# Gated cross-attention with an expert layer on one NeuronCore: another beginning, unpadded queries, context as 128 and 64 rows

## The chip, the core and the metric

The kernel runs on one core of one Trainium2 chip. The time is the device time of one execution in microseconds; the kernel before takes 589.01 us (median of three runs, 587.1 to 589.69). The profile is one further execution, taken with the hardware profiler. TensorE multiplies matrices, VectorE (DVE) reduces and combines, ScalarE (ACT) applies functions and copies, GpSimd (POOL) does small work and indirect DMA, SyncE (SP) issues DMA.

## The reference

For 16 sequences of 112 tokens of 256 numbers, and for each a context of 375 rows of 192 numbers:

```python
x = x + tanh(g_xattn) * xattn(layernorm(x), ctx, mask, Wq, Wk, Wv, Wo)
x = x + tanh(g_ffn) * ffn(layernorm(x), router_w, gate_w, gate_b, up_w, up_b, down_w, down_b)

# xattn: 16 heads of 16 numbers
q, k, v = x @ Wq, ctx @ Wk, ctx @ Wv            # split into heads
attn = softmax(where(mask, q @ k.T * 16**-0.5, -max))
return (attn @ v) @ Wo

# ffn: 8 experts of 512, the best two for each token
probs = softmax(x @ router_w.T)                  # two largest kept, made to sum to 1
h = silu(x @ gate_w[e] + gate_b[e]) * (x @ up_w[e] + up_b[e])
return sum over the two of probs[e] * (h @ down_w[e] + down_b[e])
```

All is float32.

## The kernel before

**Batches.** The main loop takes step i = 0 to 15, one for each batch, as a pipeline: step i holds the keys of batch i + 1, the values and score maxima of batch i, the scores, exponentials and weighted sums of batch i - 1, and the projection, second norm and routing of batches i - 2 to i - 4. The list `order` (L670) writes the order of these pieces down, `first_order` (L711) that of step 0; before them stands a prologue (L681 to L710). All engines but POOL run in the written order (`manual_schedule`, L164), so a waiting instruction holds up everything behind it on its engine, DMA issues included.

**Heads in row groups.** A head has 16 numbers. In `k_sb` and in the query tile `q1` each head has 32 rows: 16 of data, row 16 for the row maximum, row 17 for the mask. Four heads lie above each other, in four groups (NG). A score product has 32 rows, and products on different 32-row groups of TensorE run at the same time.

**Keys** (L362) are `wk.T @ context`, with the 192 context rows as two pieces of 96 (CC): for each half of the heads two products. ScalarE copies the result to `kc`, and eight DMAs spread its heads to their 32-row places in `k_sb` (three buffers; their other rows are filled once, by `set_keys`, and the mask rows by `masks`). **Values** (L386) are three products of 125 context positions, also in two pieces of 96 rows. **Queries** (L330) use `wqp`, the query weights with each head padded to 32 columns, so that the product comes out in its 32-row places; VectorE adds `row_mask` as it evicts it.

**Maxima and scores.** `maxima` (L403) multiplies keys and queries, and VectorE reduces each pair of heads to row maxima in `mt`. `q_less_max` (L426) transposes `mt` on TensorE and subtracts it from the queries, so that the next product needs only an exponential. `scores` (L443) gives the transposed scores, and ScalarE their exponential. `both` (L466) merges a unit of scores of one batch with a unit of maxima of the next. Each unit takes one of two buffers (`ps_s`). So two such groups follow each other no sooner than the exponential and the reduction of the first are done; pieces between them are TensorE's cover. All other products share three PSUM buffers (`ps_m`), which go around.

**Memory queues.** `fetch(i)` (L652) puts the loads of a later context, mask rows and tokens on SP, and two expert weight loads of 512 KB on ScalarE's queue. `load_more` (L201) loads the gates, `wo`, router and biases and clears two buffers; the tanh of the gates (L851) is the first ScalarE instruction of step 1. Eight semaphores tell of landed DMAs of both queues; a DMA that is given one in use waits for the landing of the earlier DMA.

**Experts.** Tokens are sorted into blocks of 128 for one expert. Twelve blocks (NA) from the first 11 batches are planned inside the loop, the rest at the end of the attention by `plan_rest` (28 small VectorE steps, L950). The blocks' work is a list of pieces: for each block `begin` (gate product, turn of the next block), `up`, and `others` (lists, gathers, `down` of two blocks before, `turn_h` of one before). `blocks(n)` (L1163) runs the next n pieces; between them stands the rest of the attention, and at L1231 the plan, ten steps and then one piece. After it come the lists of blocks 12 to 15 and their gathers.

## Time and profile before

| what | value |
|---|---|
| median of three runs | 589.01 us (587.1 to 589.69) |
| profiled execution | 583.11 us, span 581.3 us |
| mean granted TensorE clock | 0.986 |
| TensorE busy | 541.6 us, 93% of the span |
| VectorE, ScalarE, POOL busy | 353.4, 215.5, 143.4 us |
| DMA | 64.49 MB, 111 GB/s |
| first reduction of score maxima | at 23.11 us |
| transposes of batch 0's maxima (step 1), of batch 6's and 7's | at 34.42, 184.00 and 205.61 us |

The span is the time from the first to the last instruction. A line of a timeline gives the start in the span, the time that the merged instructions cover, the engine (a q behind it: its sequencer, which issues DMAs), the line of the kernel, the operation, the tiles (result, then operands), the number of instructions, and in brackets how long the engine had been idle and what released it. A float32 product shows as two TensorE passes. A group's line gives busy time, the mean ns of one instruction, and the idle time before it.

### The profile page before, as it was taken

What the parts mean: (1) busy time and instruction counts of PE and PEld (TensorE: products, weight loads), DVE (VectorE), ACT (ScalarE), POOL (GpSimd) and SP (SyncE); (2) the same over time, 40 slices, a digit from 0 to 9 for tenths busy, and PEclk for the clock granted to TensorE, in tenths of its full rate; (3) what the DMA queues carried; (4) which work ended last, traced back from release to release, by engine and by line L of the source; (5) the groups of instructions that cost most, each with busy time, mean ns of one, the idle gap of its engine ahead of it and who ended that gap; (6) DMA issues with size and microseconds to landing.
All of it is one profiled execution on the core that took longest, in us unless ns stands there. A gap on an engine that the chain in (4) does not pass through costs nothing. (4 is left out here: it accounts for less than half of the span.)

```text
span 581.3 us, 13620 instructions
## 1 busy us (share of the span) xinstructions
PE 541.6 (93%) x5159; PEld 381.8 (66%) x5159; DVE 353.4 (61%) x883; ACT 215.5 (37%) x391; POOL 143.4 (25%) x187
## 2 busy tenths in 40 slices
PE   3999999999999999999999999999979999999990
PEld 2567777777777777777776676666546666666660
DVE  4464656676676677666666765566884646464640
ACT  2334443533533533443444344423223333333320
POOL 6000000210210210110110123254543354425432
PEclk9999999999999999999999999999979999999996
DMA  4355244244154154144211107555645566677421
GB/s 116 83 149 138 63 140 127 45 137 133 39 139 133 39 137 127 42 124 131 52 38 42 37 11 226 134 118 108 155 101 166 147 167 144 176 244 189 91 27 21
DMA packets 45810, 64.49 MB, mean 111 GB/s; under 512 B 12456, under 2 KB 36464, under 8 KB 45680
## 3 DMA queue, kind: packets, MB, share of 16 engines
q1 hardware_dynamic: 29152, 41.79, 25.1%
q0 software_dynamic: 7168, 8.42, 9.8%
q10 hardware_dynamic: 9424, 13.38, 7.5%
q8 instruction: 43, 0.70, 0.5%
q14 instruction: 23, 0.19, 0.1%
HBM read 48.87 MB, written 10.01 MB: 101 GB/s over the span
## 5 line engine op out<-in xcount | busy, mean ns | idle before, releaser
L420 DVE TENSOR_REDUCE mt<-s 112x2 f32<-112x750 f32 x128 | 118.5, 938 | 72.3 <-PE s L411 72.0
L462 ACT ACTIVATE pt<-st 125x896 f32<-125x896 f32 x96 | 88.0, 917 | 111.5 <-PE s L411 108.3
L411 PE MATMUL s<-k,q 32*112 32x375 f32 x512 | 125.2, 518 | 0.4 <-DVE mt L420 0.2
L452 PE MATMUL st<-q,k 32*125 32x112 f32 x1536 | 108.2, 279 | 9.0 <-DVE mt L420 5.5
L452 PEld LDWEIGHTS st<-q,k 32*125 32x125 f32 x1536 | 91.2, 183 | 28.3 <-DVE mt L420 15.9
L1042 DVE TENSOR_TENSOR gu<-gu,b 128x512 f32<-128x512 f32 x64 | 41.3, 686 | 70.3 <-PE gu L1026 70.3
L1081 PE MATMUL pd<-wd,hT 128*128 x256 | 62.7, 389 | 3.7 <-ACT hT L1073 3.7
L1081 PEld LDWEIGHTS pd<-wd,hT 128*128 128x128 f32 x256 | 49.4, 195 | 22.5 <-issue 11.9
L636 POOL DMA_INDIRECT routed<-ent,slot x32 | 31.1, 971 | 128.5 <-DVE slot L632 123.7
L1026 PE MATMUL gu<-wg,xT 128*128 x128 | 61.2, 601 | 0.2 <-issue 0.2
L411 PEld LDWEIGHTS s<-k,q 32*112 32x112 f32 x512 | 54.8, 170 | 9.5 <-DVE mt L420 7.5
L1026 PE MATMUL gu<-wu,xT 128*128 x128 | 60.6, 596 | 0.0
L297 POOL TENSOR_TENSOR rstd<-ve,mhalf 112x1 f32<-112x1 f32 x32 | 18.4, 574 | 160.7 <-DVE ve L295 160.7
L390 PE MATMUL vp<-wv_sb,c 96*125 96x256 f32 x192 | 52.6, 396 | 0.0
L368 PE MATMUL kp<-c,wk_sb 96*128 96x375 f32 x128 | 49.3, 512 | 0.0
L1051 ACT ACTIVATE sg<-gu 128x512 f32<-128x512 f32 x32 | 20.2, 631 | 74.8 <-DVE gu L1042 74.8
L482 PE MATMUL o<-pt,v 125*32 125x112 f32 x1536 | 46.8, 262 | 0.0
L482 PEld LDWEIGHTS o<-pt,v 125*32 125x32 f32 x1536 | 35.2, 110 | 13.9 <-issue 13.7
L838 POOL DMA_INDIRECT x<-normed,toks x32 | 32.6, 1017 | 34.0 <-issue 22.9
L390 PEld LDWEIGHTS vp<-wv_sb,c 96*125 96x125 f32 x192 | 33.2, 187 | 9.8 <-issue 6.1
L1026 PEld LDWEIGHTS gu<-wg,xT 128*128 128x128 f32 x128 | 22.5, 194 | 16.7 <-issue 16.6
L1026 PEld LDWEIGHTS gu<-wu,xT 128*128 128x128 f32 x128 | 21.9, 191 | 15.4 <-issue 15.4
(170 smaller groups left out, 654.9 us busy)
## 6 DMA issues: line engine op xcount, KB each, us to landing
b<-bias_d SPq DMA_DIRECT2D x32, 640.0 KB
k<-kc SPq DMA_DIRECT2D x124, 46.9 KB
c<-in_ctxT_dram SPq DMA_DIRECT2D x32, 140.6 KB
wg<-in_gate_w_dram ACTq DMA_DIRECT2D x8, 512.0 KB
wu<-in_up_w_dram ACTq DMA_DIRECT2D x8, 512.0 KB
wd<-in_down_w_dram ACTq DMA_DIRECT2D x8, 512.0 KB
xs<-in_x_dram SPq DMA_DIRECT2D x16, 112.0 KB
total<-xs SPq DMA_DIRECT2D x16, 112.0 KB
```

Source lines behind the costliest of these rows:

```text
L368: nc.tensor.matmul(ps[:, :M], lhsT=wk_sb[:, k, j * 128 : (j + 1) * 128], rhs=c[:, k, :], start=(k == 0), stop=(k == 1),)
L390: nc.tensor.matmul(ps[:KC, :D], lhsT=ct[:, k, c * KC : (c + 1) * KC], rhs=wv_sb[:, k, :], start=(k == 0), stop=(k == 1),)
L411: nc.tensor.matmul(ps[:N, j, :M], lhsT=q1[rows, g, (b % 2) * N : (b % 2 + 1) * N], rhs=kt[rows, g, :], start=True, stop=True,)
L420: nc.vector.reduce_max(mt[:, g, 2 * rp : 2 * rp + 2, R_MAX], ps[:N, :, :M], axis=AX.X)
L452: nc.tensor.matmul(ps[:KC, j, g * N : (g + 1) * N], lhsT=kt[rows, g, c * KC : (c + 1) * KC], rhs=q2[rows, g, :], start=True, stop=True,)
L462: nc.scalar.activation(pt, ps[:KC, :, : NG * N], AF.Exp)
L482: nc.tensor.matmul(o[32 * r : 32 * r + 32, g * N : (g + 1) * N], lhsT=vt[:, c, 2 * g + rp, j : j + 2, :].rearrange("p t d -> p (t d)"), rh ...
L636: ins = nc.gpsimd.indirect_dma_start(out=routed, out_offset=bass.IndirectOffsetOnAxis(slot[:, k : k + 1], 0), in_=s["ent"][:, k, :], in_of ...
L838: nc.gpsimd.indirect_dma_start(out=bs[j]["x"], out_offset=None, in_=normed[: FIRST * N] if j < NA else normed, in_offset=bass.IndirectOffs ...
L1026: nc.tensor.matmul(s["ps"][:, i, :F], lhsT=s["xT"][:, k, :], rhs=w[:, bass.ds(s["e"], 1), k, :].rearrange("p o f -> p (o f)"), start=(k == 0),
L1042: nc.vector.tensor_tensor(s["gu"][:, i], s["ps"][:, i, :F], s["b"][:, i * F : (i + 1) * F], ALU.add)
L1081: nc.tensor.matmul(pd[:, :D], lhsT=s["hT"][:, f, :], rhs=wd[:, bass.ds(s["e"], 1), f, :].rearrange("p o d -> p (o d)"), start=(f == 0), st ...
```

## The change

- Context, `wk` and `wv` are loaded as 128 rows and 64 rows, and the 64 rows stand twice, in rows 0 to 63 and 64 to 127 of the tile. The last steps of two products (two halves of the keys, two chunks of values) then lie on different halves of TensorE's rows. Values are made as chunks 0 and 1 together and chunk 2 alone.
- Queries of batches 2 on use the weights as they are; VectorE copies the product, and eight DMAs a batch spread its heads. Two query buffers are filled once with `row_mask`. Batches 0 and 1 keep the padded way, with the padded weights in buffers of the exponentials.
- The prologue loads and works off keys ahead of norms, POOL too runs in the written order there, eight products of the identity with itself stand first on TensorE, `set_keys` runs on VectorE and POOL instead of ScalarE, and `load_more` moves from the prologue's end to step 1, behind its `fetch`.
- The pieces of a step stand in another order, in step 0 too.
- `plan_lanes` moves to the beginning of the last part, and the plan goes in sevens instead of tens.

```diff
-CC = C // 2
+CW = C - 128
...
+    early = ExitStack()
+    early.enter_context(tc.manual_schedule(engines={POOL}))
...
+    def load_wide(tile, rows, part, q=nc.sync):
+        if part == 0:
+            q.dma_start(out=tile[:, 0, :], in_=rows[:128])
+        else:
+            for i in range(2):
+                q.dma_start(out=tile[i * CW : (i + 1) * CW, 1, :], in_=rows[128:])
+
     def load_ctx(b):
-        c = a2.tile([CC, 2, M], F32, name=f"c_{b}", tag="c", bufs=3)
...
+        ctx_tiles[b] = a2.tile([128, 2, M], F32, name=f"c_{b}", tag="c", bufs=3)
+        for part in range(2 if b else 0):
+            load_wide(ctx_tiles[b], ctxT[b], part)
...
     load_ctx(0)
-    stage_q = ac.tile([128, KD, D], F32, name="stage_q")
-    nc.scalar.dma_start(out=stage_q, in_=wq.rearrange("(k p) d -> p k d", p=128))
-    wk_sb = ac.tile([CC, 2, D], F32)
-    nc.sync.dma_start(out=wk_sb, in_=wk.rearrange("(k p) d -> p k d", p=CC))
+    wk_sb = ac.tile([128, 2, D], F32)
+    for part in range(2):
+        load_wide(ctx_tiles[0], ctxT[0], part)
+        load_wide(wk_sb, wk, part)
     load_xa(1, nc.scalar)
-    load_ctx(1)
-    wv_sb = ac.tile([CC, 2, D], F32)
-    nc.sync.dma_start(out=wv_sb, in_=wv.rearrange("(k p) d -> p k d", p=CC))
+    wq_sb = ac.tile([128, KD, D], F32)
+    nc.scalar.dma_start(out=wq_sb, in_=wq.rearrange("(k p) d -> p k d", p=128))
+    wv_sb = ac.tile([128, 2, D], F32)
+    for part in range(2):
+        load_wide(wv_sb, wv, part, nc.scalar)
...
-    wqp = ac.tile([128, KD * H, 32], F32)
-    nc.gpsimd.memset(wqp, 0.0)
-    nc.gpsimd.tensor_copy(
-        wqp[:, :, 0:HD], stage_q.rearrange("p k (h d) -> p (k h) d", d=HD)
-    )
-
-
...
-    def set_keys(i):
-        nc.scalar.copy(
+    def set_keys(i, copy):
+        copy(
             k_sb[i].rearrange("p g m -> p (g m)"), row_max.to_broadcast([128, NG * M])
         )
...
+    set_keys(0, nc.vector.tensor_copy)
...
+    wqp = [ptp.tile([128, H, 32], F32, name=f"wqp{k}", tag="pt") for k in range(KD)]
+    for k in range(KD):
+        nc.gpsimd.memset(wqp[k], 0.0)
...
+
+    warm = ps_m.tile([128, 512], F32, name="warm", tag="m")
+    for _ in range(8):
+        nc.tensor.matmul(warm[:, :128], lhsT=ident, rhs=ident, start=True, stop=True)
...
     def queries(b):
...
         pr, u = pairs[b // 2], b % 2
-        if u == 0:
-            pr["q1"] = a2.tile([128, NG, 2 * N], F32, name=f"q1_{b}", tag="q1")
         ps = ps_m.tile([128, 512], F32, name=f"q_{b}", tag="m")
+        for k in range(KD):
+            nc.tensor.matmul(
+                ps[:, : 2 * N],
+                lhsT=wq_sb[:, k, u * 128 : (u + 1) * 128],
+                rhs=pr["xnT"][:, k],
+                start=(k == 0),
+                stop=(k == KD - 1),
+            )
+        st[b]["qc"] = a2.tile([128, 2 * N], F32, name=f"qc_{b}", tag="qc")
+        nc.vector.tensor_copy(st[b]["qc"], ps[:, : 2 * N])
+
+    def first_queries(u):
+        q1 = pairs[0]["q1"] = q_sb[0]
...
+                    lhsT=wqp[k][:, 4 * g : 4 * g + 4, :],
+                    rhs=pairs[0]["xnT"][:, k],
                     start=(k == 0),
...
+    def spread_queries(b):
+        u, qc = b % 2, st[b]["qc"]
+        q1 = pairs[b // 2]["q1"] = q_sb[b // 2 % 2]
+        for r in range(4):
+            for gh in range(2):
+                nc.sync.dma_start(
+                    out=q1[32 * r : 32 * r + HD, 2 * u + gh, :],
+                    in_=qc[64 * gh + 16 * r : 64 * gh + 16 * r + HD],
+                )
...
-        ps = ps_m.tile([128, 512], F32, name=f"kp_{b}_{j}", tag="m")
-        for k in range(2):
+        ps = st[b]["kp", j] = ps_m.tile([128, 512], F32, name=f"kp_{b}_{j}", tag="m")
+        nc.tensor.matmul(
+            ps[:, :M], lhsT=wk_sb[:, 0, j * 128 : (j + 1) * 128], rhs=c[:, 0, :],
+            start=True, stop=False,
+        )
...
+    def keys_end(b):
...
+        c = ctx_tiles[b]
+        for j in range(2):
+            rows = slice(j * CW, (j + 1) * CW)
             nc.tensor.matmul(
-                ps[:, :M],
-                lhsT=wk_sb[:, k, j * 128 : (j + 1) * 128],
-                rhs=c[:, k, :],
-                start=(k == 0),
-                stop=(k == 1),
-            )
+                st[b]["kp", j][:, :M],
+                lhsT=wk_sb[rows, 1, j * 128 : (j + 1) * 128],
+                rhs=c[rows, 1, :],
+                start=False, stop=True,
+            )
+        for j in range(2):
+            keys_out(b, j)
+
...
         if j == 1:
-            kt, kc = k_sb[b % 3], st[b]["kc"]
-            for r in range(4):
-                for gh in range(2):
-                    q = nc.scalar if b == 0 and gh else nc.sync
-                    q.dma_start(
-                        out=kt[32 * r : 32 * r + HD, gh : NG : 2, :],
-                        in_=kc[64 * gh + 16 * r : 64 * gh + 16 * r + HD],
-                    )
-
-    def values(b, c):
+            spread_keys(b, 0)
+            if b > 0:
+                spread_keys(b, 1)
+
+    def spread_keys(b, gh, q=nc.sync):
+        kt, kc = k_sb[b % 3], st[b]["kc"]
+        for r in range(4):
+            q.dma_start(
+                out=kt[32 * r : 32 * r + HD, gh : NG : 2, :],
+                in_=kc[64 * gh + 16 * r : 64 * gh + 16 * r + HD],
+            )
+
+    def values(b, chunks):
...
         ct = ctx_tiles[b]
-        ps = ps_m.tile([128, 512], F32, name=f"vp_{b}_{c}", tag="m")
-        for k in range(2):
+        pss = []
+        for c in chunks:
+            ps = ps_m.tile([128, 512], F32, name=f"vp_{b}_{c}", tag="m")
+            pss.append(ps)
+            nc.tensor.matmul(
+                ps[:KC, :D], lhsT=ct[:, 0, c * KC : (c + 1) * KC], rhs=wv_sb[:, 0, :],
+                start=True, stop=False,
+            )
+        for i, (c, ps) in enumerate(zip(chunks, pss)):
+            rows = slice(i * CW, (i + 1) * CW)
             nc.tensor.matmul(
                 ps[:KC, :D],
-                lhsT=ct[:, k, c * KC : (c + 1) * KC],
-                rhs=wv_sb[:, k, :],
-                start=(k == 0),
-                stop=(k == 1),
-            )
-        nc.scalar.copy(
-            v_sb[b % 2][:, c, :, 0:3:2, :],
-            ps[:KC, :D].rearrange("p (h t d) -> p h t d", t=2, d=HD),
-        )
+                lhsT=ct[rows, 1, c * KC : (c + 1) * KC],
+                rhs=wv_sb[rows, 1, :],
+                start=False, stop=True,
+            )
+        for c, ps in zip(chunks, pss):
+            nc.scalar.copy(
+                v_sb[b % 2][:, c, :, 0:3:2, :],
+                ps[:KC, :D].rearrange("p (h t d) -> p h t d", t=2, d=HD),
+            )
...
     order = [
-        (keys, 1, 0), (q_less_max, -1), (keys, 1, 1), (choose, -4), (queries, 2),
-        (norm_a, 5),
-        tm(0, 1), (turn_o, -2), (turn_x2, -3), (turn_x, 4),
-        tm(1, 0), (values, 0, 2), (turn_on, -2), (place, -4), (norm_b, 5),
+        (queries, 2), (keys, 1, 0), (q_less_max, -1), (keys, 1, 1), (spread_queries, 2),
+        (choose, -4), (norm_a, 5), (keys_end, 1),
+        tm(0, 1), (turn_o, -2), (values, 0, (2,)),
+        tm(1, 0), (turn_x2, -3), (turn_x, 4), (turn_on, -2), (place, -4), (norm_b, 5),
         tm(2, 3), (weighted, -1, 0), (logits, -3), (logits_exp, -3),
-        tm(3, 2), (project, -2), (values, 0, 0),
+        tm(3, 2), (project, -2),
         tm(4, 5), (weighted, -1, 1), (norm2, -2),
-        tm(5, 4), (values, 0, 1),
+        tm(5, 4), (values, 0, (0, 1)),
         (both, (maxima, 0, 6), (maxima, 0, 7)), (weighted, -1, 2),
     ]
     norm_a(0)
-    nc.vector.tensor_scalar_mul(q_scale, vps[:, :B], HD**-0.5)
     norm_a(1)
+    for k in range(KD):
+        nc.gpsimd.tensor_copy(
+            wqp[k][:, :, 0:HD], wq_sb[:, k, :].rearrange("p (h d) -> p h d", d=HD)
+        )
+    nc.vector.tensor_scalar(mb, mu, 1.0, low, ALU.subtract, ALU.mult)
     norm_b(0)
     norm_b(1)
-    nc.vector.tensor_scalar(mb, mu, 1.0, low, ALU.subtract, ALU.mult)
+    nc.vector.tensor_scalar_mul(q_scale, vps[:, :B], HD**-0.5)
     masks(0)
+    load_ctx(1)
+    keys(0, 0)
+    keys(0, 1)
+    keys_end(0)
+    turn_x(0)
+    turn_x(1)
+    spread_keys(0, 1, nc.scalar)
+    first_queries(0)
+    first_queries(1)
+    nc.gpsimd.memset(mt, 0.0)
+    for i in range(2):
+        nc.gpsimd.memset(v_sb[i], 1.0)
+    set_keys(1, nc.gpsimd.tensor_copy)
     for b in range(3, 5):
         load_xa(b)
-    turn_x(0)
-    turn_x(1)
-    keys(0, 0)
-    keys(0, 1)
     norm_a(2)
     norm_b(2)
     norm_a(3)
-    nc.gpsimd.memset(mt, 0.0)
     norm_b(3)
-    for i in range(2):
-        nc.gpsimd.memset(v_sb[i], 1.0)
     nc.gpsimd.tensor_copy(iota_e, index[:N, :E])
+    set_queries(1)
+    set_keys(2, nc.gpsimd.tensor_copy)
...
     load_xa(5)
-    set_keys(1)
-    queries(0)
-    queries(1)
+    keys(1, 0)
     fetch(0)
-    keys(1, 0)
-    keys(1, 1)
-    set_keys(2)
-    load_more()
     first_order = [
-        (both, (maxima, 0, 0), (maxima, 0, 1)), (values, 0, 0), (norm_a, 4),
-        (both, (maxima, 0, 2), (maxima, 0, 3)), (turn_x, 2), (values, 0, 1),
-        (both, (maxima, 0, 4), (maxima, 0, 5)), (turn_x, 3), (values, 0, 2), (norm_b, 4),
-        (both, (maxima, 0, 6), (maxima, 0, 7)), (queries, 2), (turn_x, 4), (norm_a, 5),
-        (norm_b, 5),
+        (both, (maxima, 0, 0), (maxima, 0, 1)), (keys, 1, 1), (keys_end, 1),
+        (both, (maxima, 0, 4), (maxima, 0, 5)), (values, 0, (0, 1)), (norm_a, 4),
+        (both, (maxima, 0, 2), (maxima, 0, 3)), (turn_x, 2), (turn_x, 3), (values, 0, (2,)),
+        (norm_b, 4),
+        (both, (maxima, 0, 6), (maxima, 0, 7)), (queries, 2), (spread_queries, 2),
+        (turn_x, 4), (norm_a, 5), (norm_b, 5),
     ]
         if i > 0:
             fetch(i)
         if i == 1:
+            load_more()
             nc.scalar.activation(tg, gates, AF.Tanh)
...
     fetch(B)
+    plan_lanes()
     choose(B - 4)
...
     choose(B - 1)
-    plan_lanes()
     blocks(2)
     place(B - 1)
     plan_taken()
     blocks(1)
     steps = plan_rest()
-    for i in range(0, len(steps), 10):
-        for step in steps[i : i + 10]:
+    for i in range(0, len(steps), 7):
+        for step in steps[i : i + 7]:
             step()
-        if i + 10 < len(steps):
+        if i + 7 < len(steps):
             blocks(1)
     for j in range(4):
         load_list(NA + j)
```

## The prediction

> **What bounds the kernel now.** I read the page first, then TensorE's timeline of one step of the batch loop, then the waits around the two places where TensorE is not full. The page: TensorE is at work nearly everywhere; slice 30 is the only one inside with a lower clock (slice 1 shows full clock, but its passes are slow, below).
>
> ```profile
> PE   3999999999999999999999999999979999999990
> PEclk9999999999999999999999999999979999999996
> L368 PE MATMUL kp<-c,wk_sb 96*128 96x375 f32 x128 | 49.3, 512 | 0.0
> L390 PE MATMUL vp<-wv_sb,c 96*125 96x256 f32 x192 | 52.6, 396 | 0.0
> ```
>
> Each float32 matmul is recorded as two passes: 64 key products give x128. In the timeline of one middle step the reader sees that it is a chain of TensorE work (182.63 to 204.24, 21.6 us) with one wait, 0.27 us for VectorE:
>
> ```profile
> 182.63 1.53 PE L368 MATMUL kp<-c,wk_sb 96*128 96x375 f32 x4
> 184.00 0.55 PE L429 MATMUL mt<-ident,mt 112*128 112x112 f32 x4
> 184.38 1.44 PE L368 MATMUL kp<-c,wk_sb 96*128 96x375 f32 x4
> 185.66 1.68 PE L338 MATMUL q<-xnT,wqp 128*128 128x224 f32 x8
> 187.27 0.36 PE L452 MATMUL st<-q,k 32*125 32x112 f32 x2
> ...
> 189.70 0.36 PE L452 MATMUL st<-q,k 32*125 32x112 f32 x2 [0.27 <-DVE mt L420]
> ...
> 201.31 1.13 PE L390 MATMUL vp<-wv_sb,c 96*125 96x256 f32 x4
> 202.42 0.99 PE L411 MATMUL s<-k,q 32*112 32x375 f32 x8
> ```
>
> At the beginning SyncE's queue sets the pace (what it issues, and when):
>
> ```profile
> 18.48 2.71 SPq L381 DMA_DIRECT2D k<-kc  x4
> ...
> 26.02 5.20 SPq L381 DMA_DIRECT2D k<-kc  x8
> 31.26 0.58 SPq L202 DMA_DIRECT2D gates<-in_g_xattn_dram  x1
> 31.89 0.44 SPq L203 DMA_DIRECT2D gates<-in_g_ffn_dram  x1
> ```
>
> and ScalarE waits behind it, since the tanh of the gates stands in its order before everything of step 1:
>
> ```profile
> 35.50 0.20 ACT L851 ACTIVATE tg<-gates 128x2 f32<-128x2 f32 x1 [1.71 <-DMA gates<-in_g_ffn_dram]
> ```
>
> Where the expert plan is worked out, TensorE waits 3.0 us, and then works at half clock (eight passes take 3.6 us at 429.30 and 1.7 at 420.31):
>
> ```profile
> 420.31 1.89 PE L1081 MATMUL pd<-wd,hT 128*128 x8
> ...
> 429.30 3.78 PE L1081 MATMUL pd<-wd,hT 128*128 x8 [3.00 <-ACT hT L1073]
> 432.87 1.06 PE L1069 MATMUL ht<-ident,h 128*128 128x128 f32 x4
> 433.72 2.66 PE L1026 MATMUL gu<-wg,xT 128*128 x4
> ```
>
> **The change, 1: the plan.** VectorE works off 28 plan steps as 10, 10 and 8 (417.19 to 427.02, with one y of 0.4) ahead of the next block's bias sum; ScalarE has that block's tanh ahead of the hT that TensorE waits for. In sevens, 21 steps stand before the bias sum; the last seven (reduce 0.57, cast 0.1, 0.57, 0.57, 0.28, 0.2, 0.06) come to 2.3 us. So the wait of 3.0 us falls to 0.7 to 0.9. A TensorE wait of 1.3 us at 410.6 left the clock at full, so I take the half clock out too: pd, ht and gu take 6.9 us from 429.30 and 3.9 at full clock, 3.0 us. Late next: the gathers of blocks 12 on are issued one piece nearer their use; a gather takes 3.9 us to land, and I charge 0.7. Sum: 2.2 + 3.0 - 0.7 = 4.5 us off; bounds 0 (the gather takes it all) and 6.2 (no new wait). The three plan_lanes instructions, 0.15 us each, move to where TensorE has work: nothing, at most 0.4.
>
> **2: the step's TensorE work.** Per pass 0.315 (keys), 0.215 (values), 0.20 us (queries), from starts in the timeline. Keys: 8 passes become 4 of full height and two shared pairs, 6 in time: 0.63. Values: 12 become 6 full, one pair, one alone: 10 in time, 0.43. Queries: 8 become 4: 0.80. In all 1.86 us a step if pairs run together; rows for it are the scores, where two 32-row heads start 7 ns apart (176.349 and 176.356), each pass pair 0.11 us after the last. But three more 64-row stretches stand between full and 32-row ones. A change of height costs, in the rows, 0.26 us going to full (values start at 190.83, 0.16 after the scores' last pass, and their first pass takes 0.32) and 0.18 going back; for 64 rows no row exists; between 0 and 0.26 I take 0.18.
>
> What reaches the step's end is less, because waits take the place of work. From the step's start: queries 0.9 (first pass 0.1 longer), keys 0.63, so the maxima's transposes start at 1.54 and VectorE's subtraction at 2.12 (184.00 to 184.59 is 0.585). From it to the reduction after the first score group VectorE needs 4.13 us now (184.59 to 188.72); without the padded queries' eviction (0.60) 3.53, so the second group starts at 2.12 + 3.53 + 0.985 = 6.64, against 7.07 now, whatever TensorE saves (it would be there at 6.3, which also hides the 0.18s of the first two stretches). Gain 0.43. Then turn_x2, turn_x, turn_on and place want four of three PSUM buffers in a row: place waits for the copy of x2, which ScalarE does after the exponential (1.36 + 0.81 + 0.30 after the group's start). Third group at 9.51 against 9.76: gain 0.25. Values 0 leave the stretch behind project, 0.96 us, of which exponential and reduction (1.36 + 0.88 from group to group) let 0.81 through: gain 1.06. The statistics behind project then delay the next reduction by 0.17: 0.89. Values 0 and 1 in one stretch take 0.6 more before the last maxima (0.97 + 0.61 + 0.13 after the group's 1.13, against 2.23): 0.29 left. Nine steps at 0.29, three (11 to 13: no norm, no turn_x) at 1.1, two at 0.45: 6.8, taken as 6.5 us. Bounds: 9.5 with free changes of height; 3 us slower where pairs run one after the other (0.43 of values and 0.27 of keys a step, fourteen times).
>
> Eight DMAs for queries and one for context join each step. SyncE's issues, from their rows (0.43 context, 0.6 masks and keys, 0.35 to 0.45 others): about 13.5 us of 21.6, before 9.7; keys are due a step later, so nothing. Without that cover: see the third rival. VectorE's unpadded eviction hides in its wait before 184.59.
>
> **3: the beginning.** Keys go first, so their spreading does not wait for norms. The first maxima reduction is at 23.11 now. Context and wk come as 640 KB on SyncE (480 now, landed at 7.0): keys about 8; masks, context 1 and spreads issue from about 7 to 13.5 (4 x 0.65, 3 x 0.43, 4 x 0.65) and land 2.2 later; then VectorE wants xa of batch 3, which is issued behind the spreads: norm 3 (0.4 + 0.2 + 0.15 + 0.66 + 0.4) ends at about 18. So the first reduction is at 18 (16.5 to 20), 5 us early. Four pairs at 2.75 (27.00 to 29.77), paced by VectorE, as now: batch 2's queries are copied at about 29.
>
> What is late next: the gates. Their loads now stand behind spread_queries(2), which waits for that copy, and behind step 1's fetch: 8 x 0.4 + 3 x 0.43 + 4 x 0.6 + 2 x 0.4 = 7.7 us, then 1.0 for themselves, landing 2 (an xa) to 3.5 us (31.89 to 35.44) later. ScalarE's tanh thus at 40 to 42 against 35.50, and behind it wait both key evictions (0.47 each), the first exponential, and TensorE, for the key's PSUM buffer. Second group of step 1 at about 42.3 (39.5 to 44.5) against 40.37: the 5 us are gone, and 2 more. TensorE would idle some 7 us before. The rows at 429 show that a wait of 3 us brought half clock for 6.8 us and cost 3.0; in step 1 exponentials hide half: 1.5.
>
> The Trainium skill's page TensorE: Matmul & The Clock Gate (section Why this matters for your kernels) asks for about 4 us of busy TensorE to reach full clock and for no idle gap over about 3 us. The eight identity products suit its first half, the gates' wait breaks its second. Its window of 3.4 us at half clock would make the estimate 1.7 us lost at most, where this trace has 3.0.
>
> POOL now follows the written order too: the two wqp copies, the memsets, the key fill of batch 1, then the powers of norms 2 and 3, the query fill, the key fill of batch 2. By 0.61 us for 512 columns a key fill (1500) takes 1.7 and a query fill (896) 1.0. Batch 1's rows are filled at about 12.5, and SyncE wants them for masks at 17; all is done at 20. ScalarE loses two copies of 1.44 that it had time for; batch 0's fill goes to VectorE, before xa lands. Covered, so nothing; without that cover 1 us on norm 3. Behind the gates on SyncE stand wo and six small loads, of which rwT waited 4.4 us for a weight load, then queries 3 and keys 2 (16 issues): landed at about 56, due at about 60.
>
> The warm-up: cold key passes take 0.63 us (eight from 10.40 to 15.43), warm ones 0.33 (18.46 on). Eight products are 16 passes of about 0.21 cold, 3.4 us in time that was idle; nothing is behind them but keys that wait for DMA. It is worth up to 2 us and lies under the same gate wait. Sum of 3: 3.5 us longer; bounds 5 shorter (no wait on the gates) and 7 longer.
>
> **Sum** on the profiled execution, 583.11 (span 581.3): - 4.5 - 6.5 + 3.5 = -7.5, 575.6. The median of the runs is 589.01, 5.9 above it: 581.5.
>
> **Rivals.** (a) The gates don't hold: the front keeps its 5 us. For it: ScalarE waited only 1.7 us for them; against: the issue list above. 573. (b) The step gains nothing, VectorE and ScalarE taking all 1.86 us: they have 0.27 us of waits to show for now, but most groups already follow at 2.23, the least that exponential and reduction allow. -4.5 + 3.5: 588. (c) Slower: SyncE becomes the bound. It waits in order, and in the trace its key spreads already waited on landings of the weight loads (L381 on wd, wu, wg: 5.8 us in six waits, rwT 4.4 in one). With 13.5 us of issues it decides once such waits pass 8 us a step; 2 us beyond, in the twelve steps with weight loads, is 24: 605. Against it: two loads of 6 us a step, partly at once. (d) Pairs run in series: -4.5 + 3 + 3.5, 591.
>
> **How the numbers follow.** Mine 0.52, with its own range 577 to 587; (a) 0.18; (b) 0.13; (c) 0.07; (d) 0.10. A measurement here can tell about 0.5% from no change: 586.1 to 592.0. Faster: 0.47 of mine, 0.18 of (a), 0.02 of (b): 0.67. Same: 0.05, 0.10 and 0.05 of mine, (b) and (d): 0.20. Slower: 0.13. 571 to 592 leaves out most of (c) and a tail of (a) and (d).
>
> **What would show it.** Right: tanh of gates after 38 with a wait of over 5 us, TensorE idle before; first reduction near 18; steps of about 21.3 us with kp x6 or a wait at place on the x2 copy; no pd wait over 1.5 us and no half clock in the plan. Wrong: steps under 20.8 or over 21.8 us; 64-row passes of a pair starting 0.2 us apart; SyncE waiting in every step; the gates landed by 36.

## The result, and the profile after

The changed kernel takes 597.6 us (median of 19 runs, 591.8 to 608.2), the kernel before 589.7 us on the same chip (19 runs, 584.8 to 595.3). The ratio is 1.0103, 95% interval 1.0068 to 1.0139: 6 us slower, where 581.5 was forecast (571 to 592). All ratios leave out executions in a slower state, in which the time is longer at a lower clock; the medians and ranges keep them. The two profiled executions lie further apart, 597.56 us (span 595.9) and 583.11 us (581.3), since the latter is at the fast end of its runs.

The transposes of a batch's maxima (a batch is "turned" when they start) divide the span into three parts. The second profile of the changed kernel, taken with the experiments, has fewer half-clock windows in the loop:

| | before | after | after, again | forecast |
|---|---|---|---|---|
| batch 0 turned at | 34.4 us | 35.6 | 35.4 | |
| batch 1 turned at | 54.7 | 71.1 | 70.7 | |
| beginning, to batch 1 | | +16.3 | +16.0 | +3.5 |
| loop, batch 1 to batch 15 | 297.1 | 290.5 | 287.5 | |
| | | -6.6 | -9.6 | -6.5 |
| batch 15 to the end | 229.5 | 234.3 | 235.0 | |
| | | +4.8 | +5.5 | -4.5 |

The page of the profile after, TensorE in 40 slices: the second slice is at a lower clock, the fourth mostly idle and at half clock, and the row of the loop is as full as before.

```profile
PE   7773999999999999999999989999998999999960
PEclk9695999999998999899999999999998999999995
```

Groups of instructions of the profile after: keys and values had 128 and 192 passes, 49.3 and 52.6 us; now they are four groups of 93.2 us together.

```profile
L408 PE MATMUL kp<-c,wk_sb 128*128 128x375 f32 x64 | 26.2, 493 | 1.8 <-DVE qc L360 1.8
L418 PE MATMUL kp<-c,wk_sb 64*128 64x375 f32 x64 | 15.6, 551 | 1.0 <-DMA wk_sb<-in_wk_dram 1.0
L450 PE MATMUL vp<-wv_sb,c 128*125 128x256 f32 x96 | 28.6, 408 | 0.0
L456 PE MATMUL vp<-wv_sb,c 64*125 64x256 f32 x96 | 22.8, 438 | 0.0
```

One middle step, from TensorE's timeline: four key passes of 64 rows take 0.90 us, since two run at once; the waits for VectorE (0.19) and, at `place`, for the copy of x2 (0.64). The step is 21.15 us long (197.91 to 219.06), 0.45 less.

```profile
197.28 0.79 PE L408 MATMUL kp<-c,wk_sb 128*128 128x375 f32 x2
197.91 0.55 PE L495 MATMUL mt<-ident,mt 112*128 112x112 f32 x4
198.30 0.81 PE L408 MATMUL kp<-c,wk_sb 128*128 128x375 f32 x2
199.04 0.90 PE L418 MATMUL kp<-c,wk_sb 64*128 64x375 f32 x4
...
202.90 0.36 PE L518 MATMUL st<-q,k 32*125 32x112 f32 x2 [0.19 <-DVE mt L486]
...
205.46 0.36 PE L684 MATMUL pos<-sel,ahead 112*112 112x8 f32 x2 [0.64 <-ACT x L628]
```

SyncE's queue at the beginning, after: the spreading of batch 2's queries cannot be issued before 35.34, takes 7.23 us (4.8 of issues and 2.4 of waits for expert weights), and the gates' loads stand at 48.04, where they stood at 31.26.

```profile
23.16 5.24 SPq L438 DMA_DIRECT2D k<-kc  x8
35.34 7.23 SPq L388 DMA_DIRECT2D q<-qc  x8
42.67 0.53 SPq L173 DMA_DIRECT2D c<-in_ctxT_dram  x1
43.24 1.15 SPq L176 DMA_DIRECT2D c<-in_ctxT_dram  x2
44.49 2.56 SPq L397 DMA_DIRECT2D k<-mb  x4
47.09 0.44 SPq L185 DMA_DIRECT2D xa<-in_x_dram  x1
47.58 0.42 SPq L189 DMA_DIRECT2D xs<-in_x_dram  x1
48.04 0.43 SPq L212 DMA_DIRECT2D gates<-in_g_xattn_dram  x1
48.51 0.43 SPq L213 DMA_DIRECT2D gates<-in_g_ffn_dram  x1
```

ScalarE's timeline: the tanh waits 17.24 us (1.71 before), and the key evictions and the first exponential of step 1 follow it. The bracket names the router's load, which begins to land at that moment; the tanh's own last wait is for the second gate load, issued at 48.51 and landed at 52.00.

```profile
52.09 0.20 ACT L926 ACTIVATE tg<-gates 128x2 f32<-128x2 f32 x1 [17.24 <-DMA rwT<-in_routerT_dram]
52.34 0.85 ACT L429 COPY kc<-kp 128x375 f32<-128x375 f32 x2
53.07 0.94 ACT L528 ACTIVATE pt<-st 125x896 f32<-125x896 f32 x1
```

TensorE stands still meanwhile, from 42.02 to 54.06, and is at half clock until 60.59. Three stretches of the changed kernel; the columns are the stretch and its length, the busy time of PE, PEld, DVE, ACT and POOL with their counts, the granted clock, the DMA share and GB/s:

```profile
17.00:30.00 13.00, 10.21 (x36) 4.47 (x36) 7.41 (x11) 1.49 (x4) 3.49 (x5) 0.61 0.41 101
42.00:52.00 10.00, 0.03 (x2) 0.00 (x0) 0.00 (x0) 0.00 (x0) 0.00 (x0) 0.58 0.35 86
52.00:61.00 9.00, 6.47 (x81) 5.17 (x84) 2.20 (x3) 4.31 (x8) 0.00 (x0) 0.52 0.27 68
```

Before, the clock is 1.00 in all three stretches and TensorE is busy for 9.74 us of the second. The Trainium skill's page TensorE: Matmul & The Clock Gate (section Why this matters for your kernels) warns of idle gaps of over about 3 us; the trace agrees here, with a granted clock of 0.52 behind a gap of 12.04 us.

At the plan, TensorE's timeline after: the wait of 3.00 us is 0.61 and its passes are at full clock, but the turn of block 12 now waits 3.09 us for its gather, and the up product behind it runs at half clock (3.56 us, 1.88 elsewhere).

```profile
436.43 1.99 PE L1156 MATMUL pd<-wd,hT 128*128 x8 [0.61 <-ACT hT L1148]
...
444.51 1.88 PE L1101 MATMUL gu<-wg,xT 128*128 x4
449.49 0.48 PE L1083 MATMUL bx<-ident,x 128*128 128x128 f32 x2 [3.09 <-DMA x<-normed,toks]
449.76 3.56 PE L1101 MATMUL gu<-wu,xT 128*128 x4
453.15 1.89 PE L1156 MATMUL pd<-wd,hT 128*128 x8
```

And the end, which no step of the prediction looked at. The blocks' scatters on POOL's timeline, before:

```profile
568.22 1.55 POOL L1098 DMA_INDIRECT out_dram<-y,toks  x1 [2.97 <-issue]
572.81 1.55 POOL L1098 DMA_INDIRECT out_dram<-y,toks  x1 [3.04 <-DMA out_dram<-y,toks]
```

and after:

```profile
573.59 1.57 POOL L1173 DMA_INDIRECT out_dram<-y,toks  x1 [3.98 <-DVE sg L1132]
578.13 1.56 POOL L1173 DMA_INDIRECT out_dram<-y,toks  x1 [2.97 <-DVE y L1164]
582.65 1.55 POOL L1173 DMA_INDIRECT out_dram<-y,toks  x1 [2.96 <-issue]
587.16 1.55 POOL L1173 DMA_INDIRECT out_dram<-y,toks  x1 [2.95 <-DMA out_dram<-y,toks]
```

Each scatter adds to the same tensor and waits until the one before it has landed: the starts are 4.5 to 4.6 us apart. (A bracket names what came last by the profile, which need not be that landing.) The last y is made at 568.08 before and 577.26 after: the last scatter follows it by 4.7 us before and by 9.9 after. What TensorE gains stands in front of a queue that is late.

### The profile page after: what moved, and what is told of

It is laid out like the page before. It is cut to its first block, busy times and chain, and to the rows that moved or that the text cites. A ratio compares the mean times of both kernels' runs of the same rounds, so it can differ in the third digit from the quotient of the medians.

```text
span 595.9 us, 13777 instructions
## 1 busy us (share of the span) xinstructions
PE 533.0 (89%) x5119; PEld 359.4 (60%) x5119; DVE 348.4 (58%) x884; ACT 207.3 (35%) x388; POOL 151.1 (25%) x192
## 5 line engine op out<-in xcount | busy, mean ns | idle before, releaser
L477 PE MATMUL s<-k,q 32*112 32x375 f32 x512 | 127.2, 538 | 16.1 <-ACT pt L528 12.0
L518 PE MATMUL st<-q,k 32*125 32x112 f32 x1536 | 111.8, 284 | 9.0 <-DVE mt L486 7.4
L518 PEld LDWEIGHTS st<-q,k 32*125 32x125 f32 x1536 | 94.1, 188 | 35.3 <-DVE mt L486 22.2
L1101 PE MATMUL gu<-wu,xT 128*128 x128 | 62.3, 610 | 0.0
L1156 PE MATMUL pd<-wd,hT 128*128 x256 | 60.9, 381 | 1.4 <-ACT hT L1148 1.4
L548 PE MATMUL o<-pt,v 125*32 125x112 f32 x1536 | 49.0, 270 | 0.0
L548 PEld LDWEIGHTS o<-pt,v 125*32 125x32 f32 x1536 | 37.0, 113 | 14.3 <-issue 14.0
L429 ACT COPY kc<-kp 128x375 f32<-128x375 f32 x32 | 13.6, 475 | 49.4 <-PE kp L418 49.3
L1173 POOL DMA_INDIRECT out_dram<-y,toks x12 | 19.7, 1640 | 40.2 <-DVE h L1134 13.4
L1173 POOL DMA_INDIRECT total<-y,toks x12 | 20.3, 1688 | 35.7 <-DVE gu L1117 15.2
```

The costliest lines, as they stand in the source:

```text
L477: nc.tensor.matmul(ps[:N, j, :M], lhsT=q1[rows, g, (b % 2) * N : (b % 2 + 1) * N], rhs=kt[rows, g, :], start=True, stop=True,)
L518: nc.tensor.matmul(ps[:KC, j, g * N : (g + 1) * N], lhsT=kt[rows, g, c * KC : (c + 1) * KC], rhs=q2[rows, g, :], start=True, stop=True,)
L548: nc.tensor.matmul(o[32 * r : 32 * r + 32, g * N : (g + 1) * N], lhsT=vt[:, c, 2 * g + rp, j : j + 2, :].rearrange("p t d -> p (t d)"), rh ...
L1101: nc.tensor.matmul(s["ps"][:, i, :F], lhsT=s["xT"][:, k, :], rhs=w[:, bass.ds(s["e"], 1), k, :].rearrange("p o f -> p (o f)"), start=(k == 0),
L1156: nc.tensor.matmul(pd[:, :D], lhsT=s["hT"][:, f, :], rhs=wd[:, bass.ds(s["e"], 1), f, :].rearrange("p o d -> p (o d)"), start=(f == 0), st ...
L1173: nc.gpsimd.indirect_dma_start(out=dest, out_offset=bass.IndirectOffsetOnAxis(to, 0), in_=y, in_offset=None, compute_op=ALU.add,)
```

## The experiments

The first four ran on a chip on which every kernel is slower (before: 600.5 us median), so their traces are read by their waits and their times by the ratio only.

### The beginning: gates, weights, SyncE

```diff
@@ the first run: load_more() back ahead of the first step
         fetch(0)
+        load_more()
         first_order = [
...
             if i == 1:
-                load_more()
                 nc.scalar.activation(tg, gates, AF.Tanh)
```

> load_more() goes back ahead of the first step, behind fetch(0); all else as in the changed kernel. Theory (the gates are late: tanh waited 17.2 us on ScalarE, and TensorE stood behind the exponentials queued after it): the wait falls under 3 us, the maxima of batch 1 are turned at 55 to 58 instead of 71.06, and the time falls by 13 to 16 us, to about 583. Rival A (the loads wait for the memory, wherever they are issued, because the weights of the experts and the queries' spreading fill it): the wait stays above 8 us and the gain is under 6 us. Rival B (the end is set by the chain of scatters on POOL, which started late for a reason of its own): the gain is under 10 us although batch 1 is turned 14 us earlier.

Measured: ratio 1.0176 (1.0055 to 1.0298). The tanh no longer waits, batch 1 is turned at 60.8 us, but the next step takes 27.6 us and batch 3 is turned at 108.4 (111.8 in the changed kernel): 3 us are left of 10, compared across chips. What took the gates' place is in the waits of SyncE's queue (total, times, longest, in us):

```profile
SPq L438 <- DMA wg<-in_gate_w_dram: 7.0, 1, 7.0
```

Eight semaphores tell of landed DMAs of SyncE and ScalarE alike. The fifth DMA that spreads batch 1's keys has the same one as an expert's weights (number 107 in the trace for both), which ScalarE's queue had not issued yet: SyncE stood from 30.7 to 37.8.

```profile
34.06 0.39 ACTq L101 DMA_DIRECT2D wg<-in_gate_w_dram  x1
```

Half of the theory held (the gates were late), its price did not. Rival A falls, as the wait is gone. Rival B is not tested, since most of the gain is lost again by batch 3, far ahead of the scatters.

The two gates alone:

```diff
+        def load_gates():
+            nc.sync.dma_start(out=gates[:, 0:1], in_=g_xattn.partition_broadcast(128))
+            nc.sync.dma_start(out=gates[:, 1:2], in_=g_ffn.partition_broadcast(128))
...
         fetch(0)
+        load_gates()
         first_order = [
```

> Only the two loads of the gates go ahead of the first step, behind fetch(0); the other seven of load_more() stay in step 1. Theory (the two gates alone hold ScalarE): the same as with all nine moved, 13 to 16 us less than the changed kernel, about 583. Rival C (wo, the router's weights and the rest, late by themselves, hold the projection and the logits of batch 0 in steps 2 and 3): batch 1 is turned at 55 to 58, but steps 2 or 3 get a wait of over 2 us and the gain is 8 to 12 us.

Measured: 605.4 to 621.1 us, too far apart for a ratio with an interval. Batch 1 is turned at 55.4, and the step after it takes 31.8; batch 3 at 107.2. The gates alone hold ScalarE in step 1, as the theory had it; the loss comes back a step later, larger than rival C had it, by waits of SyncE's queue (5.3 us for the queries' copy, 2.3 for weights).

The changed kernel as it is, for the next chip:

> The changed kernel itself, unaltered, so that the other three have it on their own chip. Every theory: about 1.01 times the kernel before; batch 1 turned at 69 to 72, batch 3 at 110 to 113.

Measured: 595.3 us, ratio 1.0099 (1.0046 to 1.0152); batch 1 at 70.7, batch 3 at 111.5.

The weights later, on top of the first run:

```diff
-            if i >= 1:
+            if i >= 3:
                 for _ in range(2):
                     if bulk:
                         bulk.pop(0)()
```

> As the first run (load_more() ahead of the first step), and the weights of the experts, two loads a step on ScalarE's queue, begin at step 3 instead of step 1. In the first run the gates no longer held ScalarE, but SyncE stood 7.0 us ahead of the fifth spreading DMA of batch 1's keys, released by the landing of an expert's weights that ScalarE's queue issued at 34.06: the two share a completion semaphore. Theory (that sharing holds SyncE in steps 1 and 2): SyncE's waits for weights are gone, batch 1 is turned at 53 to 56, batch 3 at 96 to 100 instead of 108.4, and the time is 8 to 12 us less than the first run's, as a ratio to the kernel before 0.998 to 1.004. Rival F (SyncE has simply too many issues in steps 0 to 2, with or without the sharing): batch 3 is turned after 104 and the ratio stays above 1.008.

Measured: 583.1 us, ratio 0.9934 (0.9882 to 0.9987), against 1.0099 of the changed kernel on the same chip: 1.65% of the kernel before. Batch 1 is turned at 56.3, batch 3 at 98.2 (97.4 before): the loss of the beginning is gone but for 0.8 us, and the kernel is faster than both. SyncE's eight key spreads now go through:

```profile
27.86 6.43 SPq L438 DMA_DIRECT2D k<-kc  x8
35.07 4.99 SPq L388 DMA_DIRECT2D q<-qc  x8
```

They took 12.82 us in the first run:

```profile
27.45 12.82 SPq L438 DMA_DIRECT2D k<-kc  x8
```

The fourth combination, which is this diff alone on the changed kernel:

> The changed kernel with the expert weights from step 3, and load_more() left in step 1. Theory (two causes in a row, each enough: the gates hold ScalarE in step 1, and when they don't, the shared semaphores hold SyncE): tanh still waits 12 to 16 us, batch 1 is turned at 66 to 70 instead of 71, batch 3 at 107 to 111, ratio 1.003 to 1.010. Rival O (the weights alone were the cause): tanh waits under 8 us, batch 3 turned before 102, ratio below 0.999.

Measured: tanh waits 15.0 us, batch 1 at 68.4, batch 3 at 109.2; ratio 1.0192 (1.0056 to 1.0328, few runs), above the 1.003 to 1.010 expected, with an interval that reaches into it. Rival O falls.

```profile
48.59 0.20 ACT L926 ACTIVATE tg<-gates 128x2 f32<-128x2 f32 x1 [15.00 <-DMA gates<-in_g_ffn_dram]
```

The first run's kernel once more:

> The first run's kernel (load_more() ahead of the first step, weights from step 1) again, on the chip of the others. Theory: SyncE waits about 7 us for a weight load ahead of the fifth spreading DMA of batch 1's keys, batch 1 is turned at 59 to 62, batch 3 at 106 to 110, ratio 1.004 to 1.010, hardly better than the changed kernel. If on this chip the wait is gone: batch 3 before 102 and ratio below 1.0.

Measured: ratio 1.0027 (0.9975 to 1.0080), better than expected; batch 1 at 64.0, batch 3 at 104.7. SyncE waits 5.4 us for the weights (7.0 on the other chip), ScalarE for the spreading behind it:

```profile
40.75 0.85 ACT L429 COPY kc<-kp 128x375 f32<-128x375 f32 x2 [6.90 <-DMA k<-kc]
```

So batch 3 is turned at 111.5 us with neither mended, 109.2 with the weights alone, 104.7 with the gates alone, 98.2 with both. With the gates alone the executions differ: the fourth run, whose beginning is the same, has batch 1 at 64.3 and batch 3 at 105.0, the first run 60.8 and 108.4. Two causes in a row: mending the first shows the second.

The same bytes on another queue:

```diff
-            bulk += load_w(e)
+            bulk += load_w(e, nc.gpsimd if e < 2 else nc.scalar)
```

> As the first run (load_more() ahead of the first step, expert weights from step 1), with the six loads of the first two experts on POOL's queue, whose completions have semaphores of their own: the same bytes at the same steps. Theory (the weights hold SyncE because they share its eight completion semaphores): SyncE waits for no weights, batch 3 is turned at 96 to 100, ratio 0.990 to 0.998, as with the later weights. Rival L (the weights hold the rest by the bytes that they move): batch 3 is turned after 104, SyncE or the spreading DMAs land late, ratio above 1.005.

Measured: ratio 0.9967 (0.9929 to 1.0004). SyncE waits for no weights, and steps 1 to 3 take 61.1 us (62.8 with the later weights, 76.1 in the changed kernel). But POOL did not keep to the steps: it issued the first weights at 4.65 us, and batch 0 was turned 8.3 us later, at 43.7. So this doesn't tell the semaphore from the bytes as it should have; for the semaphore speak its number, the same on both queues, and the waits, which end as the weights land.

### The rest of the beginning

All that the traces named, at once:

```diff
-            nc.sync.dma_start(out=gates[:, 0:1], in_=g_xattn.partition_broadcast(128))
+            nc.scalar.dma_start(out=gates[:, 0:1], in_=g_xattn.partition_broadcast(128))
...
         first_queries(1)
+        load_more()
...
         masks(0)
+        for b in range(3, 5):
+            load_xa(b)
         load_ctx(1)
...
-        set_keys(2, nc.gpsimd.tensor_copy)
+        set_keys(2, nc.scalar.copy)
```

All nine loads of load_more() go to ScalarE's queue, set_queries(1) to ScalarE as well; in each step spread_queries stands behind keys_end, and the weights begin at step 3.

> All that the traces name for the beginning: load_more() on ScalarE's queue behind the first queries, x of batches 3 and 4 issued ahead of the keys' spreading, the third key tile and the second query tile filled by ScalarE instead of POOL, keys' spreading ahead of the queries' in each step, expert weights from step 3. Theory (the beginning lost its time on SyncE's queue and on VectorE's wait for the norms of batch 3 and for POOL): first reduction at 17 to 19 instead of 22.6, batch 0 turned at 29 to 32, batch 3 at 90 to 95 instead of 111.8; 16 to 20 us less than the changed kernel, ratio to the kernel before 0.975 to 0.985. Rival F: SyncE still holds step 2 and batch 3 is turned after 100; ratio above 0.99. Rival B (the chain of scatters at the end does not follow): batch 15 is turned 16 us earlier, but the end gains under 12.

Measured: ratio 0.9973 (0.9921 to 1.0024); first reduction at 23.9, batch 0 at 36.8, batch 3 at 98.9. A miss: ScalarE, which now filled the query tile, stood 9.8 us behind load_more() on its own queue. On top of the run with the later weights, with x and the copies as above but load_more() on SyncE, and the steps' order left:

```diff
         first_order = [
             (both, (maxima, 0, 0), (maxima, 0, 1)), (keys, 1, 1), (keys_end, 1),
+            (lambda b: load_more(), 0),
```

> As the run with the later weights, and: x of batches 3 and 4 issued on SyncE ahead of batch 1's context, the third key tile and the second query tile filled by ScalarE, load_more() behind the spreading of batch 1's keys. Theory (the first reduction waits for the norm of batch 3, which waits for its x behind the keys' spreading, about 2.3 us, and for POOL's two copies of 0.93 and 1.44 us, during which VectorE's norm takes 2.50 us instead of 0.41): the norm takes 0.4 us, the first reduction comes at 17.5 to 19.5 instead of 22.7, batch 0 is turned at 31 to 33 instead of 35.4, and the time falls by 2.5 to 4.5 us, ratio 0.985 to 0.990. Rival M (the norm is not held by POOL's copies): it still takes 2.5 us. Rival N (what is gained ahead of batch 0 is lost to the keys or queries of batches 1 to 3, that is to SyncE): batch 3 is turned after 97 as before, ratio 0.992 to 0.996.

Measured: ratio 0.9890 (0.9794 to 0.9985, five runs). The first reduction comes at 19.25 and batch 0 is turned at 31.9, as expected. VectorE's timeline of the changed kernel:

```profile
18.70 0.43 DVE L308 BATCH_NORM_STATS2 stats<-xa 112x6 f32<-112x256 f32 x1 [1.88 <-DMA xa<-in_x_dram]
...
20.20 2.50 DVE L317 TENSOR_SCALAR xn<-xa,mv,rstd 112x256 f32<-112x256 f32 x1 [0.66 <-POOL rstd L314]
22.62 1.77 DVE L486 TENSOR_REDUCE mt<-s 112x2 f32<-112x750 f32 x2
```

and with the early norms:

```profile
16.54 0.42 DVE L308 BATCH_NORM_STATS2 stats<-xa 112x6 f32<-112x256 f32 x1
...
18.03 0.41 DVE L317 TENSOR_SCALAR xn<-xa,mv,rstd 112x256 f32<-112x256 f32 x1 [0.66 <-POOL rstd L314]
19.25 1.79 DVE L486 TENSOR_REDUCE mt<-s 112x2 f32<-112x750 f32 x2 [0.80 <-PE s L477]
```

The norm of batch 3 is 0.41 us instead of 2.50 without POOL's copies beside it, and its x is there 2.2 us earlier. Rival M falls. Rival N has a part in this execution: step 2 takes 26.3 us (21.9 with the later weights), the next one 22.8 with a half-clock window, and batch 3 is turned at 101.9; in the run with this beginning and tens (below) at 95.9.

Without the eight products of the identity, on the run with the later weights:

```diff
-        warm = ps_m.tile([128, 512], F32, name="warm", tag="m")
-        for _ in range(8):
-            nc.tensor.matmul(warm[:, :128], lhsT=ident, rhs=ident, start=True, stop=True)
```

> As the run with the later weights, without the eight products of the identity with itself at the start. Theory (they raise the granted clock at 5.97 us, yet it falls back at about 29.5 us for 10.2 us, since TensorE is idle too long from 18.8 on; what they gain ahead of that is under 1 us, because the first reduction waits for the norms of batch 3): batch 0 turned within 1 us of 35.4, the time within 2 us, ratio 0.990 to 0.997. Rival K (the products are what makes the beginning as short as it is): batch 0 turned after 37, ratio above 0.997.

Measured: ratio 0.9941 (0.9895 to 0.9986), batch 0 at 35.8: no difference from 0.9934. The products are worth nothing measurable here, where the first reduction waits for the norm of batch 3. (The expectation's 29.5 us is not counted from the span's start: there the clock of the run with the later weights is full from 5.36 to 19.01 us and then half for 10.24.)

### The plan and the end

The plan in tens, in the changed kernel, then with the loads early, then with the beginning of the two runs above:

```diff
-        for i in range(0, len(steps), 7):
-            for step in steps[i : i + 7]:
+        for i in range(0, len(steps), 10):
+            for step in steps[i : i + 10]:
...
-            if i + 7 < len(steps):
+            if i + 10 < len(steps):
```

> The plan's steps in tens again instead of sevens (plan_lanes stays early). Theory (the gain at the plan was taken by the later gathers of blocks 12 to 15): the wait of the turn of block 12 falls from 3.09 us to under 0.5, the wait of the down product ahead of the plan rises from 0.61 to 2.5 to 3.5, and the time changes by less than 2 us, about 597. Rival D (the sevens put all the gathers and scatters on POOL back, and the chain of scatters sets the end): 3 to 5 us less than the changed kernel, about 593.5. Rival E (the sevens are worth the 4.5 us forecast): 3 to 5 us more, about 602.

Measured: ratio 1.0221 (1.0131 to 1.0311), on the slower chip, where the changed kernel itself was not run; no verdict between the rivals. The waits came as the theory had them: none at the turn of block 12, 3.3 us at the down product.

> Both: load_more() ahead of the first step and the plan in tens. Theory: the two act apart, so the first run's gain with the third's change on it: 13 to 16 us less than the changed kernel, about 583. Rival D: 16 to 19 us less, about 580. Rival E: 9 to 12 us less, about 587.

Measured: ratio 1.0177 (1.0080 to 1.0273), the first run's 1.0176: tens and sevens alike.

> The same with the plan's steps in tens again. Theory: within 2 us of the one with sevens, either way, since the wait of the turn of block 12 (3.09 us) comes and goes against the wait of the down product (3.0 us). Rival D (the sevens put POOL's scatters back and they set the end): 3 to 5 us less. Rival E: 3 to 5 us more.

Measured: 0.9949 (0.9889 to 1.0009) against 0.9973 with sevens: the same within the intervals, as the theory had it.

> The same with the plan's steps in tens. Theory (the end is the chain of scatters, which is set by what it loses at the plan): the last scatter comes 0.5 to 2 us earlier after the turn of batch 15's maxima than with sevens (225.0 there, 223.7 in the run with tens), ratio 0.001 to 0.003 lower. Rival: no difference beyond 0.001.

Measured: 582.1 us, ratio 0.9926 (0.9886 to 0.9967), against 0.9890 (0.9794 to 0.9985) with sevens: not told apart. The last scatter comes 225.0 us after the turn of batch 15's maxima, 224.6 with sevens: the theory's 0.5 to 2 us are not there. Of the runs that compute everything, four have intervals below 1: later weights, no identity products, early norms, and this one.

The plan's part of the change alone, in the kernel before:

```diff
         fetch(B)
+        plan_lanes()
...
-        plan_lanes()
...
-        for i in range(0, len(steps), 10):
+        for i in range(0, len(steps), 7):
```

> The kernel before with the plan alone of the change: steps in sevens, plan_lanes at the blocks' start. The forecast gave this 4.5 us: ratio 0.992. Theory (the end is set by the chain of the blocks' scatters on POOL: each waits until the one before it has landed, at 4.6 us or more, in the traces 5.7 to 5.8 us apart over blocks 8 to 19, which is TensorE's own 5.82 us a block, so that what the chain loses once at the plan it never makes up, and what TensorE gains there is not seen): TensorE's last down product comes 0.5 to 1.5 us earlier, the last scatter 2 to 4.5 us later, ratio 1.003 to 1.008. Rival H (the chain catches up): within 1 us, ratio 0.998 to 1.002.

Measured: ratio 1.0035 (0.9978 to 1.0091). The 4.5 us that I forecast would be 0.992, outside the interval. The interval also holds rival H, so it is the traces that tell. Starts, counted from the first down product, to leave out what lies ahead (us; "y" is the last block's sum on VectorE):

| | last down product | last y | last scatter | end |
|---|---|---|---|---|
| before | 186.6 | 188.7 | 193.4 | 201.9 |
| before, with sevens | 186.1 | 188.2 | 198.1 | 206.7 |
| changed kernel, again | 185.1 | 187.2 | 198.8 | 207.4 |
| later weights (sevens) | 186.0 | 188.1 | 197.4 | 206.0 |
| early norms, tens | 185.5 | 187.6 | 197.4 | 205.7 |
| less TensorE work | 179.8 | 181.9 | 195.5 | 204.2 |
| half of the last scatters | 186.3 | 188.4 | 189.2 | 200.9 |

TensorE is done 0.5 us earlier, the scatters 4.7 later: close to the theory's 0.5 to 1.5 and 2 to 4.5. In the profile before, the scatter of block 8 is issued 3.8 us behind its down product, with sevens 12.5; by block 18 it is still 7.9 behind (5.2 before), since from there the chain needs what TensorE needs for a block, 5.8 us. The time is lost in one landing: the scatter of block 7 lands 3.7 us after its issue before (58.15 to 61.82) and 8.2 us after it with sevens (56.72 to 64.90), and the scatter of block 8, whose y has been there since 58.94, follows at 65.70. In that time two gathers, a bias load and the load of a list are issued, before only the bias load; what slows the landing is not shown.

The other order of scatter and gather on POOL:

```diff
+            if 0 <= j - 2:
+                down(j - 2)
             if LEAD <= ahead_j < NA or NA + 4 <= ahead_j < LAST:
                 gather(ahead_j)
-            if 0 <= j - 2:
-                down(j - 2)
```

> As the run with the later weights (ratio 0.9934), and in each block the scatter of block j-2 is written ahead of the gather of block j+4 on POOL's queue. Theory (the scatters' chain sets the end, and the gather ahead of each scatter delays its issue and its landing): the last scatter comes 221 to 223 us after the turn of batch 15's maxima instead of 225.0, 2 to 4 us less time, ratio 0.987 to 0.990. Rival I (the chain is paced by landings, and a gather later by one scatter lands beside the next): no change, 0.991 to 0.996. Rival J (the gathers come too late and the turns wait): ratio above 0.996, with waits of the turns of over 1 us.

Measured: ratio 0.9967 (0.9908 to 1.0026). Over blocks 8 to 18 the scatters come as in the run with the later weights (rival I); at the copy from `total` to `out` the gathers now stand behind the scatter that waits for it, and the down products jump by 8.6 us there (rival J).

Less work for TensorE in the last blocks:

```diff
+            last = 1 if i == 1 and j >= FULL else KD
-            for k in range(KD):
+            for k in range(last):
...
-                    stop=(k == KD - 1),
+                    stop=(k == last - 1),
```

> As the run with the later weights, with one of the two halves of the up product's sum left out in the last twelve blocks (j >= FULL), so that TensorE has 0.87 us less work in each of them, 10.4 us in all; the output of those blocks is not the reference's. Theory (the chain of scatters on POOL sets the end): the last down product comes 8 to 10 us earlier, the last scatter less than 1.5 us earlier, ratio 0.990 to 0.994. Rival (TensorE sets the end): the last scatter and the end 7 to 10 us earlier, ratio 0.975 to 0.982.

Measured: ratio 0.9852 (0.9782 to 0.9922). From 10.4 us less work TensorE gains 6.2 (at one block it waits 1.98 us behind VectorE, which waits 5.15 for the load of a list, and a half-clock window follows), the last scatter 1.9, the end 1.7 in the profiled execution; by the ratios against the run with the later weights it is 4.8 us, with intervals that overlap. So neither the theory's "less than 1.5 us" nor the rival's 7 to 10 came, and how much of TensorE's gain reaches the end is not told.

Half of the last scatters (those with an even j - FULL are left out, so half of what these blocks add is missing):

```diff
-            nc.gpsimd.indirect_dma_start(
+            if j < FULL or (j - FULL) % 2:
+                nc.gpsimd.indirect_dma_start(
```

> As the run with the later weights (ratio 0.9934), with every second scatter of the last twelve blocks left out (j >= FULL and j - FULL even), so that half of what these blocks add is missing from the output. Theory (the chain of scatters sets the end): the last scatter follows the last y by under 2 us instead of 9.4, and comes 7 to 10 us earlier after the turn of batch 15's maxima (215 to 218 instead of 225.0), ratio 0.976 to 0.982. Rival (TensorE sets the end): less than 2 us, ratio above 0.989.

Measured: ratio 0.9803 (0.9706 to 0.9901). The last scatter follows the last y by 0.8 us and comes 8.3 us earlier, with TensorE as late as ever:

```profile
555.92 1.55 POOL L1174 DMA_INDIRECT out_dram<-y,toks  x1 [7.14 <-DVE y L1164]
563.64 1.55 POOL L1174 DMA_INDIRECT out_dram<-y,toks  x1 [6.16 <-DVE y L1164]
```

The end gains 5.1 us in the profiled execution, as from the last scatter to the end it takes 11.7 us instead of 8.5: POOL's closing drain takes 7.41 us instead of 4.88, why is not shown. So the chain of scatters does set the end, by about 5 us here.

## Why the prediction was wrong

The two profiled executions lie 14.5 us apart, with -7.5 forecast. Of the 22.0 us between, 12.8 are the beginning's, 9.3 those of the plan and the end.

**The beginning (+3.5, measured +16).** The mechanism (the gates hold ScalarE, and TensorE behind it) was right and the size was off by a factor of over four; this is the term that decided, and within it SyncE's queue. Its parts:
- "The first reduction is at 18": 22.62. SyncE's key spreads began at 13.16 and batch 3's x, behind them, was issued at 16.50, where I had them done by 13.5; then the norm took 2.50 us, not 0.4, beside POOL's copies, which I had called covered, with 1 us for the case that they are not. The run with the early norms gave 19.25.
- "Batch 2's queries are copied at about 29": 34.90. The reductions of the score groups start 3.5, 4.3 and 2.8 us apart instead of 2.75, in part at half clock (0.61 from 17 to 30).
- "8 x 0.4 + 3 x 0.43 + 4 x 0.6 + 2 x 0.4 = 7.7": from 35.34 to 48.04 it is 12.7. A spreading DMA of queries takes SyncE 0.6 us, as my own rows had it for keys, and two waits for weights add 2.4. So the tanh at 52.09, not 40 to 42.
- "Due at about 60" for batch 2's keys: late as soon as the gates are not. Waits for weights on shared semaphores I saw in the trace before, but priced them only as a loss in every step (rival c); they decide in the first two, where SyncE has no slack.

**The loop (-6.5, measured -6.6 and -9.6).** Right in mechanism: pairs of 64-row passes run together, `place` waits for the copy of x2 (0.64), steps of 21.15. That the first profile has 6.6 is partly chance: two of its steps take 22.7 us with a half-clock window. The second, without, gives 9.6, about my bound of 9.5: the gain is 0.5 us in a middle step instead of 0.29. Rivals (b) and (d) fall.

**The plan (-4.5, alone measured +0.35%).** The wait fell to 0.61 (0.7 to 0.9 forecast) and the half clock behind it went, as forecast. The term that failed first is "I charge 0.7" for the gathers: 3.09 us of wait and a half-clock window, my bound "the gather takes it all". (The other bound, 6.2, doesn't follow from its terms either: 2.2 and 3.0 make 5.2.) What failed altogether was to take TensorE's time for the end's: no step asked what follows the last down product. In the trace before one scatter still waited for another behind the last y, so the chain had no room; the tens of the experiments don't get the 4 us back either. What makes the chain lose its time at blocks 6 to 8 I have not shown: with sevens it is the landing of block 7's scatter, with tens block 6's lands 1 to 2 us later than before. One rival is untested: every run that lost the time also has `plan_lanes` early, the one with sevens in the kernel before included, and no run moves it back. I had priced that move at nothing, at most 0.4 us.

**The warm-up** was worth nothing, as its cover was forecast to make it.

Of what was to show it: tanh after 38 with a wait of over 5 us, steps near 21.3, the wait at `place` and no wait of over 1.5 us at a down product came; the first reduction near 18 and a plan without half clock did not.

## What to carry to other kernels

When loads are moved behind other issues on one queue, price the whole queue from its own rows, waits for shared completion semaphores included, and then do it again with the first cause mended: the next one stands right behind it. Before crediting a gain of the busiest engine, follow the chain that ended last from the end back: where the last instructions are serial DMAs with their landings, the engine's gain stays in front of them.
